# The start of a decoder kernel: constants and first loads as operations of its graph, and low-rank weights in two arrays

## The chip, the core and the metric

The kernel runs on one core of a Trainium2 chip. Its time is the device time of one execution in microseconds, the median of the runs shown. A lower time is better.

## What is computed

The reference is a decoder of four layers on `x` (4 x 256 x 128) with a context (4 x 512 x 96). Twelve stages each add their output to `x`. Two of them stand at the start and are touched by the change: `attn0` (one head of self-attention) and `X0` (cross-attention to the context with 16 heads, low-rank additions to its four weights, and four image tokens with keys and values of their own).

```python
def _L0_xattn_ref(x, context, Wq, Wk, Wv, Wo, bo, q_down, q_up, q_alpha, ...):
    def _lora(t, down, up, alpha):
        return t @ down @ up * (LORA_W * alpha[0] / RANK)
    q_in = x @ Wq + _lora(x, q_down, q_up, q_alpha)
    org_ctx = context[:, :end, :]
    ipa_ctx = context[:, end:, :]
    k_in = org_ctx @ Wk + _lora(org_ctx, k_down, k_up, k_alpha)
    v_in = org_ctx @ Wv + _lora(org_ctx, v_down, v_up, v_alpha)
    out = _attention(q_in, k_in, v_in)
    out = out + IPA_SCALE * _attention(q_in, ipa_ctx @ Wk_ipa, ipa_ctx @ Wv_ipa)
    return out @ Wo + bo + _lora(out, o_down, o_up, o_alpha)
...
    x = x + _L0_attn_ref(_layernorm(x, axis=-1), L0_attn_W, L0_attn_b)
    x = x + _L0_xattn_ref(_layernorm(x, axis=-1), ctx_768, ...)
    x = x + _L0_ffn_ref(_layernorm(x, axis=-1), ...)
    ...
```

The other stages are two feed-forward nets and a mixture of experts, two attentions with small heads, a wide causal attention, an attention from latents, a net with quantised weights, one more single head (`attn3`) and one more wide cross-attention (`X3`), and at the end `F3`, six layers of local attention and feed-forward.

## The kernel before

`Decoder.prepare` and the start of `Net.run` issue by hand, ahead of everything else: the transfers of `x` (four, SP's queue), of `cols`, `rows` and `ctxT` (ACT's queue), of the mask (SP), and on POOL the identity, the causal masks, the band masks, the zeroed tiles `pads`, `vs` and `vb` and the selection pattern `pick16`. `Net.prepare` fills those tiles with memsets.

All else is a graph. A stage calls `op(name, fn, reads, writes, holds)`; the name gives the engine, a weight and a due time from the table `NET` (or `LOCAL` for F3). A planner, `Flow.order`, runs a list schedule: it keeps a time per engine, takes the operation that can start first, and among those that can start takes the one with the earliest due time. The result is one fixed order of instructions for each engine; each engine works its list strictly in that order and waits by semaphores. `LAGS` gives how long an operation's result needs to its readers. Where PE would stand idle for a while, the planner puts in turns of the identity matrix (`keep`), whose result nobody reads; the first such group, `warm`, has `WARM` turns. So three kinds of PE instruction carry line 412: turns of data, keep-warm turns and `warm`.

All working tiles are cut out of one tensor, `arena`, by kinds: `w4` (1024 columns, seven slots) for the wide weights, `x4` (four slots), `e2` (five), `h` (two), `kx`, `qx` and so on. A `fetch` (L426) is a transfer on SP's queue into such a slot, and waits for the slot's last users. Hardware transfers share eight completion semaphores in turn, so the ninth waits for the first.

The head of the order, in words, with the lines of before:

- `n_stats` (DVE, L440 and L441), `n_eps` (DVE, L445), `n_root` (POOL, L446), `n_scale` (DVE, L456, two halves), `n_turn` (PE, L412) and a copy by ACT (L417) make the normalised and turned `x` of a batch.
- `attn0`: `h_qk` and `h_v` (PE, L409), the queries and keys with bias (DVE, L519 and L520), `h_scores`, `h_max` (DVE, L550), `h_exp` (ACT, L557), `h_turn`, `h_weigh`, `h_add` (DVE, L581). `x_bias` (POOL, L495) adds a row of `rows` to `x` before.
- `low_rank`: for each of q, k, v, o one transfer of the wide factor (32 x 1024, a slot of `x4`) and one of the narrow factor (32 x 128 or 32 x 96, a slot of `e2`); `l_scale` (DVE, L832), `l_mm` (PE, L409, 32 rows), `l_add` to the weights (DVE, L850 for q, k, v and L863 for o).
- `image_keys`: two transfers (into `x4`) and `i_kv`, sixteen matmuls of 16 columns each, then `i_out` (ACT) and `p_kimg` (POOL, L664).
- `X0` for each batch: `p_v` (eight matmuls of 512 columns, copied out by ACT and DVE), and for each pair of heads `p_k`, `p_q`, `p_scores`, `p_max` (DVE, L684), `p_exp` (ACT, L686), `p_share` (POOL, L691), `p_turn`, `p_weigh`.

The order in which stages enter the graph is the text `ORDER`; batches of one stage overlap those of the next.

Of the kernel before, what the change touches and what calls it, by code (L numbers as in the profile page):

```python
# [48 lines left out]
    ("x0_qal", 1), ("x0_kal", 1), ("x0_val", 1), ("x0_oal", 1), ("desc", 8),  # L49
# [17 lines left out]
class Decoder:  # L67
# [17 lines left out]
    def prepare(self):  # L85
# [3 lines left out]
        self.cols = c.tile([P, NCOL], F32, tag="cols", name="cols")  # L89
        self.rows = self.early.tile([P, NROW], F32, tag="rows", name="rows")  # L90
        self.x = []
        for b in range(B):
            xb = c.tile([P, 2, D], F32, tag=f"x{b}", name=f"x{b}")
            nc.sync.dma_start(out=xb, in_=self.a["x"][b].rearrange("(t p) d -> p t d", p=P))
            self.x.append(xb)
        self.load(self.cols, "cols", nc.scalar)
        nc.scalar.dma_start(out=self.rows, in_=self.a["rows"].partition_broadcast(P))
        self.ctxT = self.early.tile([CD, B, NCTX], F32, tag="ctxT", name="ctxT")
        for b in range(B):
            nc.scalar.dma_start(out=self.ctxT[:, b, :], in_=self.a["ctxT"][b])  # L100
# [4 lines left out]

        def mask(name, keeps):
            m = self.early.tile([P, 2, S], F32, tag=name, name=name)
            nc.gpsimd.memset(m, 0.0)
            for t in range(2):
                for base, q, k in keeps(t):  # L110

                    nc.gpsimd.affine_select(
                        out=m[:, t, :], in_=m[:, t, :], compare_op=ALU.is_ge, fill=NEG,
                        base=base + q * t * P, pattern=[[k, S]], channel_multiplier=q,
                    )
            return m

        self.causal = mask("causal", lambda t: [(0, 1, -1)])

        self.ident16 = self.early.tile([P, P], BF16, tag="ident16", name="ident16")  # L120
        nc.vector.tensor_copy(self.ident16, self.ident)
        self.causal16 = self.early.tile([P, P], BF16, tag="causal16", name="causal16")
        self.band16 = self.early.tile([P, 2 * P], BF16, tag="band16", name="band16")
        for m, lo, k, q in ((self.causal16, 0, -1, 1), (self.band16, 0, -1, 1), (self.band16, P, 1, -1)):
            m = m[:, lo : lo + P]
            nc.gpsimd.memset(m, 0.0)

            nc.gpsimd.affine_select(
                out=m, in_=m, compare_op=ALU.is_ge, fill=-(2.0**100), base=0, pattern=[[k, P]],
                channel_multiplier=q,  # L130
            )
# [11 lines left out]
class Flow:  # L143
# [22 lines left out]
    SETTLED = 9.0  # L166
# [179 lines left out]
class Net:  # L346
# [72 lines left out]
    def fetch(self, kind, *parts):  # L419
# [3 lines left out]
        def dma():  # L423
            for name, lo, hi, rows, view in parts:
                out = w.t[rows if isinstance(rows, slice) else slice(rows), lo:hi]
                self.nc.sync.dma_start(out=out if view is None else view(out), in_=self.a[name])  # L426

        self.op("fetch", dma, [], [w])
# [63 lines left out]
    def biased(self, b, row, reads=()):  # L492
# [3 lines left out]
            x, x, row()[:, None, :].to_broadcast([P, 2, D])), [self.x[b], *reads], [self.x[b]])  # L496


    def one_head(self, b, w, rows, scale, biased, causal):
# [63 lines left out]
        self.op("h_max", most, [sc], [nmx, pr] if causal else [nmx], [sums, pr])  # L563
# [28 lines left out]
    def pair_weights(self, names, rows):  # L592
        view = lambda x: x.rearrange("p (g m) -> p g m", m=D)
        return {
            m: self.fetch("w4", (name, 0, 1024, rows if m in "kv" else P, view if m == "o" else None))
            for m, name in zip("qkvo", names)
# [35 lines left out]
    def cross_wide(self, stage, w, bias, image=None):  # L632
# [4 lines left out]
        for b in range(B):  # L637
# [3 lines left out]
            v, vmade, vt = self.pair_values(b, w, lambda c, b=b: d.ctxT[:, b, c * P : (c + 1) * P], [], 4)  # L641
# [14 lines left out]
    def cross_pair(self, b, g, w, xT, v, vmade, vt, oT, n, image):  # L656
# [3 lines left out]
        self.op("p_k", lambda: self.mm(pk.t[:, :n], w["k"].t[:CD, cut], d.ctxT[:, b, :n]), [w["k"]], [pk], [kT])  # L660
# [83 lines left out]
    def causal_pair(self, b, g, w, xT, v, vmade, vt, oT):  # L744
# [21 lines left out]
        for e in range(2):  # L766
# [22 lines left out]
            self.op("c_max", masked, [ps2], [prob], [p, nmx])  # L789
# [29 lines left out]
    def low_rank(self, w):  # L819

        nc, d = self.nc, self.d
        parts = {}
        for i, (m, rows) in enumerate((("q", D), ("k", CD), ("v", CD), ("o", RANK))):

            r = slice(RANK * i, RANK * (i + 1))
            low, high = ("down", "up") if m != "o" else ("up", "down")
            n = rows if m != "o" else D
            big = self.fetch("x4", (f"x0_{m}{high}", 0, 1024, r, None))
            small = self.fetch("e2", (f"x0_{m}{low}", 0, n, r, None))

            def scale(m=m, small=small, n=n, r=r):
                nc.vector.tensor_scalar(  # L832
                    small.t[r, :n], small.t[r, :n], d.col(f"x0_{m}al")[r], 1.0 / RANK, ALU.mult, ALU.mult,
                )

            self.op("l_scale", scale, [small], [small])
            parts[m] = big, small, r, rows
        for h in range(2):
            cut = slice(h * 512, (h + 1) * 512)
            made = {m: self.buf("bank") for m in "qkv"}  # L840

            def products(made=made, cut=cut):
                for m, ps in made.items():
                    big, small, r, rows = parts[m]
                    self.mm(ps.t[:rows, :], small.t[r, :rows], big.t[r, cut])

            self.op("l_mm", products, [b for m in "qkv" for b in parts[m][:2]], list(made.values()))
            for m, ps in made.items():
                n = parts[m][3]
                self.op("l_add", lambda m=m, n=n, cut=cut, ps=ps: nc.vector.tensor_add(  # L850
                    w[m].t[:n, cut], w[m].t[:n, cut], ps.t[:n, :]), [ps, w[m]], [w[m]])
        big, small, r, _ = parts["o"]
        for h in range(2):
# [3 lines left out]
            def product(ps=ps, h=h):  # L857
                for i in range(4):
                    g = 4 * h + i
                    self.mm(ps.t[:, i * D : (i + 1) * D], big.t[r, g * P : (g + 1) * P], small.t[r, :D])  # L860
# [5 lines left out]
    def image_keys(self):  # L866

        d, out = self.d, {}
        for m in "kv":
            wi = self.fetch("x4", (f"x0_w{m}i", 0, 1024, CD, None))  # L870
# [10 lines left out]
            self.op("i_kv", product, [wi], [ps])  # L881
# [1827 lines left out]
```

## Time and profile before

| what | us |
|---|---|
| median of 3 runs | 2117.17 (2116.97 to 2117.47) |
| the profiled execution, its own time | 2120.44 |
| span of that execution in the profile | 2118.5 |
| PE busy in the span | 2050.2 (97%) |
| DVE, ACT, POOL busy | 1638.8, 1179.3, 993.1 |
| mean granted clock of TensorE | 0.986 |

The times of a view are those of one execution, from the start of its span. A row of the timeline gives start, length, engine, line, operation, what it writes and reads, shapes and count; the bracket holds the idle time ahead of it and what ended it. A row of the windows gives the stretch, its length, then busy time and count for PE, PEld (weight loads), DVE, ACT and POOL, the granted clock of TensorE (1.00 is full speed), the share of the DMA engines and GB/s. In the chain of waits a row is start, length and what the time went to. An fp32 matmul stands as two instructions in the trace, a turn as one.

### The profile page before, as it was taken

The page shows a single profiled execution, that of the slowest core. Times are in us where ns is not written, and L with a number is a line of the kernel's source. Part 1 is how long each engine was busy: PE and PEld are TensorE (multiplying, and loading weights), DVE is VectorE, ACT ScalarE, POOL GpSimd, SP SyncE. Part 2 cuts the span into 40 slices and gives each one's busy share as a digit, 9 for nine tenths or more (in the row PEclk, how much of TensorE's full clock was granted, in tenths as well). Part 3 has the DMA queues.
Part 4 walks back from the last instruction along what each step waited for, and adds up shares of the span by engine and source line. Part 5 has one row for each costly group of instructions (what it writes and reads, how often), then busy time and mean ns, then how long its engine had stood idle before and what let it go on. Part 6 is the DMA issues. An engine that isn't in the chain of part 4 may idle for free.

```text
span 2118.5 us, 59911 instructions
## 1 busy us (share of the span) xinstructions
PE 2050.2 (97%) x24498; PEld 1373.6 (65%) x24499; DVE 1638.8 (77%) x4352; ACT 1179.3 (56%) x2668; POOL 993.1 (47%) x1155
## 2 busy tenths in 40 slices
PE   8999999999999998899999999999999999999998
PEld 6666675776675666666665666666656666666666
DVE  4767777788787668988887688789788797797882
ACT  2654727344536677566565565556556465556553
POOL 3334415231312245445364357557567465575660
PEclk8999999999999999999999999999999999999999
DMA  5000020111020000100000102112121021211101
GB/s 155 1 1 2 1 70 1 32 40 55 2 76 2 9 2 5 56 3 1 1 1 1 51 13 70 42 31 74 42 72 52 25 70 42 71 46 42 29 23 32
DMA packets 33425, 71.21 MB, mean 34 GB/s; under 512 B 5688, under 2 KB 17984, under 8 KB 33152
## 3 DMA queue, kind: packets, MB, share of 16 engines
q1 hardware_dynamic: 20320, 50.29, 8.0%
q10 hardware_dynamic: 12832, 17.09, 2.5%
q8 instruction: 194, 3.18, 0.6%
q14 instruction: 79, 0.65, 0.1%
HBM read 41.68 MB, written 0.52 MB: 20 GB/s over the span
## 4 chain that ended last, share of the span: by engine, by line
PE 68%; DVE 22%; POOL 5%; issue 3%; ACT 2%; DMA 1%; POOLq 0%; SPq 0%; ACTq 0%; DVEq 0%
PE bank L409 39%; PE bank L1828 17%; PE bank L412 9%; PE bank L2044 2%; DVE arena L1982 2%; DVE arena L1992 2%; DVE arena L1997 2%; POOL arena L2034 2%; DVE arena L1603 1%; POOL arena L1996 1%; POOL arena L2077 1%; PE bank L2118 1%; DVE arena L2085 1%; DVE arena L417 1%; DVE arena L2087 1%
## 5 line engine op out<-in xcount | busy, mean ns | idle before, releaser
L409 PE MATMUL bank<-arena 128*64 128x256 f32 (+11 forms) x6824 | 857.5, 393 | 10.5 <-ACT arena L1525 3.6
L409 PEld LDWEIGHTS bank<-arena 128*128 128x128 f32 (+4 forms) x6824 | 532.6, 165 | 276.8 <-issue 100.0
L1828 PE MATMUL bank<-arena 64*64 64x32 f32 (+3 forms) x13584 | 651.7, 251 | 6.4 <-issue 2.6
L1828 PEld LDWEIGHTS bank<-arena 64*64 64x64 f32 (+2 forms) x13584 | 387.4, 127 | 209.3 <-issue 115.9
L417 ACT COPY arena<-bank 128x512 f32<-128x512 f32 (+4 forms) x586 | 269.6, 489 | 286.1 <-PE bank L409 199.9
L1996 POOL TENSOR_TENSOR arena<-arena 128x1024 f32<-128x1024 f32 x96 | 226.7, 2364 | 124.1 <-PE bank L1828 63.4
L691 POOL TENSOR_SCALAR arena<-arena 128x508 f32<-128x508 f32 (+1 forms) x256 | 176.8, 697 | 209.2 <-DVE arena L688 184.1
L412 PEld LDWEIGHTS bank<-ident,arena 128*128 128x128 f32 x1757 | 196.6, 141 | 116.2 <-issue 47.3
L412 PE MATMUL bank<-ident,arena 128*128 128x128 f32 x1757 | 253.5, 280 | 18.3 <-DVE arena L456 8.5
L686 ACT ACTIVATE arena<-bank,arena 128x508 f32<-128x508 f32 (+1 forms) x256 | 175.3, 691 | 78.6 <-DVE arena L684 36.6
L2034 POOL TENSOR_TENSOR arena<-arena 128x1024 f32<-128x1024 f32 x96 | 180.9, 1905 | 71.8 <-DVE arena L2018 71.8
L1990 ACT ACTIVATE arena<-bank 128x512 f32<-128x512 f32 x192 | 113.9, 601 | 133.2 <-PE bank L1828 105.7
L684 DVE TENSOR_REDUCE arena<-bank 128x1 f32<-128x508 f32 (+1 forms) x256 | 164.2, 676 | 18.6 <-PE bank L409 18.4
L1002 ACT ACTIVATE arena<-bank 128x512 f32<-128x512 f32 (+1 forms) x256 | 124.6, 582 | 63.9 <-PE bank L409 62.4
L417 DVE COPY arena<-bank 128x512 f32<-128x512 f32 (+1 forms) x196 | 125.8, 667 | 42.9 <-PE bank L412 27.7
L1992 DVE TENSOR_TENSOR arena<-bank,arena 128x512 f32<-128x512 f32 x192 | 127.5, 683 | 38.0 <-ACT arena L1990 36.4
L2077 POOL TENSOR_TENSOR arena<-arena 128x1024 f32<-128x1024 f32 x48 | 91.4, 1904 | 108.5 <-ACT arena L2050 62.7
L1982 DVE TENSOR_TENSOR arena<-bank,arena 128x256 f32<-128x256 f32 x384 | 138.4, 411 | 3.1 <-ACT arena L1990 2.7
L979 DVE TENSOR_REDUCE arena<-bank 128x1 f32<-128x512 f32 (+2 forms) x256 | 116.7, 513 | 21.5 <-PE bank L409 21.1
L2050 ACT COPY arena<-bank 128x512 f32<-128x512 f32 x192 | 103.3, 601 | 28.8 <-PE bank L2044 28.7
L1997 DVE TENSOR_REDUCE arena<-arena 128x16 f32<-128x1024 f32 x96 | 114.3, 1201 | 0.0
L2044 PEld LDWEIGHTS bank<-ident,arena 128*128 128x128 f32 x768 | 87.0, 142 | 42.0 <-POOL arena L2034 21.8
(230 smaller groups left out, 2460.7 us busy)
## 6 DMA issues: line engine op xcount, KB each, us to landing
arena<-arena SPq DMA_DIRECT2D x48, 384.0 KB, 3.9
arena<-in_f_w SPq DMA_DIRECT2D x24, 512.0 KB, 3.5
arena<-in_f_wqkv ACTq DMA_DIRECT2D x18, 512.0 KB, 7.0
arena<-arena SPq DMA_DIRECT2D x48, 128.0 KB, 2.3
arena<-in_f_wo ACTq DMA_DIRECT2D x6, 512.0 KB, 4.0
arena<-in_f_w ACTq DMA_DIRECT2D x6, 341.0 KB, 3.9
arena<-in_f_w ACTq DMA_DIRECT2D x6, 192.0 KB, 6.2
arena<-in_x_wq SPq DMA_DIRECT2D x2, 512.0 KB
```

The costliest lines, as they stand in the source:

```text
L409: self.nc.tensor.matmul(out, lhsT, rhs, start=start, stop=stop)
L412: self.nc.tensor.transpose(out, in_, self.d.ident)
L417: return self.op(name, lambda: copy(out(), in_()), reads, writes, holds)
L684: self.op("p_max", lambda ps=ps, one=one: nc.vector.tensor_reduce(one(nmx), ps.t[:, :n], AX.X, ALU.max, negate=True), [ps], [most], [nmx])
L686: self.op("p_exp", lambda ps=ps, one=one, cols=cols: nc.scalar.activation(cols(), ps.t[:, :n], AF.Exp, bias=one(nmx), accum_out=one(sums)) ...
L691: nc.gpsimd.tensor_scalar(cols(), cols(), one(sums), 1.0, ALU.mult, ALU.mult)
L1828: self.nc.tensor.matmul(out, lhsT, rhs, start=start, stop=stop)
L1982: nc.vector.tensor_mul(heads(tmp.t[:, cut])[:, :, lo : lo + 32], heads(ps.t)[:, :, 32 - lo : 64 - lo], spread(1, lo, lo + 32),)
L1992: op("cosine", lambda cut=cut, ps=ps: nc.vector.tensor_mul(heads(out.t[:, cut]), heads(ps.t), spread(0, 0, 64)), [ps, w["tab"]], [out])
L1996: op("rotary", lambda: nc.gpsimd.tensor_add(out.t, out.t, tmp.t), [out, tmp], [out])
L1997: op("norms", lambda: nc.vector.tensor_reduce(ss.t[:, at : at + 16], heads(sq.t), AX.X, ALU.add), [sq], [ss])
L2034: nc.gpsimd.tensor_mul(heads(out.t), heads(out.t), rs.t[:, at : at + 16, None].to_broadcast([P, 16, 64]))
```

## The change

1. The transfers of `x`, `rows`, `ctxT` and the mask and the filling of the constants on POOL become operations of the graph (`load_x`, `load_rows`, `load_ctx`, `load_mask`, `k_causal`, `k_ident`, `k_masks`, `k_pads`, `k_values`, `k_image`, `k_pick`). The filling operations read a buffer that the `load_x` operations write, so the planner places them behind those; readers of the constants name them as buffers they read.
2. The first fetches get names and due times of their own (`load_a`, `load_low`, `load_ups`, `load_wk`, `load_ctx0`, `load_wv`, `load_wq`, `load_ctx`, `load_rows`, `load_image`, `load_wo`), with weights after their bytes. All but `cols` go to SP's queue.
3. The eight low-rank factors come in two arrays, `x0_ups` (128 x 1024) and `x0_downs` (128 x 128), with the four alphas in one column; one `l_scale` scales all four. The factors keep their 32 rows each.
4. `WARM` goes from 34 to 20, `SETTLED` from 9.0 to 8.0, and all due times of both tables and the two paces are set anew by small amounts.

```diff
-        self.x = []
-        for b in range(B):
-            ...
-            nc.sync.dma_start(out=xb, in_=self.a["x"][b].rearrange("(t p) d -> p t d", p=P))
-        self.load(self.cols, "cols", nc.scalar)
-        nc.scalar.dma_start(out=self.rows, in_=self.a["rows"].partition_broadcast(P))
-        for b in range(B):
-            nc.scalar.dma_start(out=self.ctxT[:, b, :], in_=self.a["ctxT"][b])
+        self.load(self.cols, "cols", nc.scalar)
+    def load_x(self, b):
+        self.nc.sync.dma_start(out=self.x[b], in_=self.a["x"][b].rearrange("(t p) d -> p t d", p=P))
+    def load_rows(self):
+        self.nc.sync.dma_start(out=self.rows, in_=self.a["rows"].partition_broadcast(P))
+    def load_context(self, b):
+        self.nc.sync.dma_start(out=self.ctxT[:, b, :], in_=self.a["ctxT"][b])
...
+        at = {m: slice(RANK * i, RANK * (i + 1)) for i, m in enumerate("qkvo")}
+        big = self.fetch("x4", ("x0_ups", 0, 1024, P, None), name="load_ups")
+        small = self.fetch("h", ("x0_downs", 0, D, P, None), name="load_low")
+        self.op("l_scale", lambda: nc.vector.tensor_scalar(
+            small.t[:, :D], small.t[:, :D], d.col("x0_al"), 1.0 / RANK, ALU.mult, ALU.mult), [small], [small])
...
+        begun = Buffer()
+        for b in range(B):
+            self.op("load_x", lambda b=b: d.load_x(b), [], [self.x[b], begun])
+            self.op("load_ctx" if b else "load_ctx0", lambda b=b: d.load_context(b), [], [self.context[b]])
+        self.op("load_rows", d.load_rows, [], [self.rows])
+        self.op("k_causal", d.fill_causal, [begun], [self.causal])
+        self.op("k_ident", lambda: nc.vector.tensor_copy(d.ident16, d.ident), [begun], [self.masks])
+        self.op("k_masks", d.fill_masks, [begun], [self.masks])
...
+        self.op("k_pads", empty, [begun], [b for bufs in pads.values() for b in bufs])
+        self.op("k_values", values, [begun], [self.fixed("vs", self.vss) for _ in self.vss])
+        self.op("k_image", image, [begun], [self.fixed("vb", self.vbs) for _ in self.vbs])
+        self.op("k_pick", pick, [begun], [self.pick])
+        self.op("load_mask", mask, [], [self.pick])
...
+    "load_a": ("SP", 0.8, -900.0),
+    "load_x": ("SP", 0.55, -800.0),
+    "load_low": ("SP", 0.3, -700.0),
+    "load_ups": ("SP", 2.05, -690.0),
+    "load_wk": ("SP", 1.55, -600.0),
+    "load_ctx0": ("SP", 0.8, -540.0),
+    "load_wv": ("SP", 1.55, -500.0),
+    "load_wq": ("SP", 2.05, -400.0),
+    "load_ctx": ("SP", 0.8, -300.0),
+    "load_rows": ("SP", 1.55, -250.0),
+    "load_image": ("SP", 1.55, -200.0),
+    "load_wo": ("SP", 2.05, -150.0),
+    "load_mask": ("SP", 0.9, 30.0),
+    "k_causal": ("POOL", 1.4, 43.74),
...
-LAGS = {"fetch": 6.0, "constants": 4.0, "weights": 12.0, "spread": 3.5}
+LAGS = {**{k: 2.0 for k in NET if k[:5] == "load_"}, "fetch": 6.0, "constants": 4.0, "weights": 12.0, "spread": 3.5}
...
-WARM = 34
+WARM = 20
```

The instruction lists that follow from it are these at the head. SP: `a_w`, four `x`, `x0_downs`, `x0_ups`, `x0_wk`, the first `ctxT`, `x0_wv`, `x0_wq`, three `ctxT`, `rows`, `x0_wki`, `x0_wvi`, `x0_wo`, the mask, F0's weights. POOL: the identity, `n_root` of the first batch, then memsets of `pads` (four), `vs` (two, each followed by a strided one on it, which after is L1081), `vb` (two), the masks, `pick`, the causal mask, then `x_bias`. PE: 20 warm turns, `n_turn`, `h_qk`, `l_mm` (k, v, q, first half), `l_mm` (o), `h_scores`, `l_mm` second half and o, `h_v`, one `p_k`, `h_turn`, four `p_v`, `h_weigh`, `i_kv` for k and v, three `p_v`, `n_turn` for X0, one `p_v`, one `p_k`, three `p_q`, the first `p_scores`. Before, the order was `n_turn`, `h_qk`, `h_v`, `h_scores`, 21 keep-warm turns, `h_turn`, `l_mm` both halves, `h_weigh`, 24 keep-warm turns, `l_mm` for o, `i_kv`, one `p_k`, `n_turn`, two `p_v`, one `p_q`, one `p_v`, the first `p_scores`.

## The prediction, made before the changed kernel had run

> **What bounds the kernel now.** I read the page first. TensorE fills the span, and its chain carries most of it:
>
> ```profile
> span 2118.5 us, 59911 instructions
> PE   8999999999999998899999999999999999999998
> PE 68%; DVE 22%; POOL 5%; issue 3%; ACT 2%; DMA 1%; POOLq 0%; SPq 0%; ACTq 0%; DVEq 0%
> ```
>
> The reader should see one weak slice at the start (8), two in the middle, one at the end. The change edits the start, so I read the timeline of PE from 0 to 42 us next:
>
> ```profile
> 1.59 5.92 PE L412 MATMUL bank<-ident 128*128 128x128 f32 x34 [1.59 <-POOL ident masks.py:199]
> 10.04 0.33 PE L412 MATMUL bank<-ident,arena 128*128 128x128 f32 x1 [2.52 <-DVE arena L456]
> 11.53 4.17 PE L409 MATMUL bank<-arena 128*128 128x256 f32 x12 [0.46 <-ACT arena L417]
> 15.49 2.69 PE L412 MATMUL bank<-ident 128*128 128x128 f32 x21
> 20.03 3.65 PE L409 MATMUL bank<-arena 32*128 32x512 f32 x20 [1.42 <-DVE arena L832]
> 23.51 2.78 PE L412 MATMUL bank<-ident 128*128 128x128 f32 x24
> 27.15 2.05 PE L409 MATMUL bank<-arena 32*128 32x128 f32 x16 [0.85 <-DVE arena L832]
> 29.12 8.48 PE L409 MATMUL bank<-ctxT,arena 96*128 96x16 f32 x34
> 41.94 0.70 PE L409 MATMUL bank<-arena 64*128 64x512 f32 x2
> ```
>
> The x34, x21 and x24 rows turn only the identity: keep-warm work that nobody needs. The first useful matmul is at 10.04, the low-rank products at 20.03 and 27.15, the first X0 scores at 41.94. The chain of waits for that window says why:
>
> ```profile
> 2.30 5.86 DMA x<-in_x
> 8.19 3.94 DMA ctxT<-in_ctxT
> 12.14 7.54 DMA arena<-in_x_qdown
> 19.70 0.28 DVE arena L832
> 27.15 10.45 PE bank L409 x50
> ```
>
> Transfers end three waits in a row; `q_down`, 16 KB, lands 7.54 us after its issue because the large weights stand before it. Then DVE and the windows of 3.41 us:
>
> ```profile
> 4.48 4.02 DVE L445 TENSOR_SCALAR arena<-arena 128x2 f32<-128x2 f32 x1
> 26.20:29.61 3.41, 2.56 (x22) 2.35 (x21) 3.31 (x12) 0.00 (x0) 2.12 (x3) 1.00 1.00 361
> 29.61:33.03 3.42, 3.42 (x19) 3.42 (x18) 1.11 (x2) 0.27 (x1) 0.36 (x3) 0.50 0.55 194
> 39.85:81.80 41.95, 41.95 (x222) 23.96 (x223) 29.20 (x87) 27.53 (x67) 14.91 (x44) 1.00 0.00 1
> ```
>
> L445 has a median of 159 ns over its 56 runs; here it takes 4.02 us, until POOL's run of memsets (3.85 to 8.48) pauses. The granted clock is 0.50 from 29.61 to 39.85, beside 16-column matmuls. From 39.85 to 81.80 PE is busy throughout: a loss before that is a loss at the end.
>
> **What moves in the instruction lists.** Without identity fills both kernels issue the same 14099 matmul operations. The first 201 hold the same set in another order (the 201st is reached at 81.8 us before); then the order is identical up to the 561st, and 84% of all stand in the same place. Rearranged pieces lie mainly between the 5327th and 6743rd (1192 to 1383 us) and in the last 5%. So the price is the head, carried to the end.
>
> **The head, step by step** (durations from rows of before).
> *Transfers.* Before, a_w was issued only at 6.72. Now it goes first, then four x, downs and ups: none of these seven on SP waits. Sizes in this order: a_w and cols 244 KB, x 512, downs 64, ups 512, wk 384, ctx0 192, wv 384, wq 512, three ctx 576, rows 384, wki 384, wvi 384. Before moved 137 GB/s over 0–5 us and 264 to 280 over 5–15; cumulated at these rates: downs at 5.6 us, ups 7.6, wk 9.1, wv 11.3, wq 13.2, rows 16.7, wvi 19.5.
> *First x.* Before it started DVE at 3.54, first in its queue. Behind a_w (one issue, 0.45, and 192 KB) I take 4.2; four BN rows (0.94) and L445 (0.16): 5.3. POOL is now free there: n_root 0.72, done 5.97 (before 9.30).
> *The new cover problem.* All the fills now stand directly behind n_root on POOL: four memsets of 0.25, one of 0.91, then L1081, which waits for that memset and leaves a gap. n_scale is the same kind of DVE operation that stood 4.02 us at L445. Bounds: not held, done at 7.1; held through the whole chain of fills (their rows sum to 10 us), done near 17. Value: DVE enters at gaps, as it did between the pick selects (9.34 to 10.68), so one half at 8.1, the other at the next gap, 9.3 (before 10.68). What waits for n_scale is the turn, ACT's copy and all of PE. l_scale stands behind it on DVE and gets the gap at 10.6.
> [...]
> *PE.* h_qk from 10.1 (before 11.53). The warm-up is 20 instead of 34; at 0.213 us each it ends at 5.9, PE is nearly idle until 8.1, and I expect the clock at 0.50 from 9.1 to 12.5 (before 12.5 to 16.0): h_qk 1.7, ends 11.8. Then at full clock: low-rank products half 1 with part at half clock 1.4, o-part 0.9 (8 x 0.112), scores 0.86, half 2 1.0, o-part 0.9, h_v 0.45, p_k 0.86: 18.3 with small waits for DVE. DVE beside it: l_add 0.69 each, h_max 0.69; v's last l_add ends 17.9, so the first p_v at 18.75 is just covered; a later one moves PE one for one. Then turn 0.44, four p_v 3.4, weigh 0.9: 23.1. i_kv: 32 x 0.112 = 3.6 at full clock, to 26.7; wki and wvi landed by 19.5, so 3.6 to 7 us of cover.
> DVE adds to x, takes two statistics (to 25.8), POOL copies image keys after the first i_out (25.3 to 26.0) and does two n_root (27.4); n_scale 29.1, turn 29.3, one p_v, one p_k, three p_q (0.43 each); **first scores at 32.6**, before 41.94.
> *Equal work.* Ahead of its first scores the new order has done one p_k, five p_v and two p_q more: 0.86 + 4.3 + 0.86 = 6.0 us. So 32.6 compares with 41.94 + 6.0 = 47.9: a lead of 15.3.
> *Deductions.* The clock fell after the window that held the 32-row products and stayed at 0.50 through the 16-column ones, though PE shows as busy. i_kv now fills a window of its own: one more at 0.50 costs 1.7; at least none, at most three (5.1). I take one.
> [...]
> First softmaxes now start without the stock of p_v that PE had at 42–48: some idle, 0 to 2, taken 0.6. Lead: 15.3 - 1.7 - 0.6 = **13.0 us**.
> *Edits at nothing.* Three l_scale fewer (0.26 each): DVE waited for q_down anyway. The mask transfer waits on DVE until after h_add, near 23 us, and holds F0's weights behind it on SP; before they were issued at 23.18 too and F0's first operation (L1168) stood at 117.3. x_bias waits for rows at 16.7 behind POOL's fills (to 16.1), h_add needs it at 23: cover 6. Masks, pick and causal are used only in later stages. ACT loses five issues and loads its table at once.
> *The rest.* Retuned due times move pieces in 1192–1383 us, where PE idles 7.8 us per 200. Either sign; rows say nothing on it, so -3 to +3, taken 0.
>
> **The sum.** The profiled execution took 2120.44 (span 2118.5), 3.3 above the median 2117.17. After: 2107.4 by the profiled one, and 2117.17 - 13.0 = **2104.2**. A measurement of this kernel can tell some 0.2%, 4.2 us, from no change.
>
> **Rivals.**
> 1. *DVE is held by the whole chain of fills* (row L445 for it, the pick selects against): h_qk moves from 10.1 to 17; lead 13 - 7 = 6: 2111. Chance 0.10.
> 2. *PE stays at half clock through the head*, as the 45 fills that are gone there no longer feed it: two windows more, 3.4, and up to 2 of waits: lead 8: 2109. For it: 1.68 busy of 3.42 at 9.13 was followed by 0.50. Chance 0.09.
> 3. *The lead is spent*: where DVE paces (800–900 us, DVE 92%, PE 88%), an early PE waits longer. Against: all engines keep their order there, so all shift. About 2117. Chance 0.06.
> 4. *Slower*: the rearranged piece at 1192–1383 opens a stall per repeated step. The longest wait of PE there now is 4.4 us (behind DVE L456). It decides from four such: 2104.2 + 17.6 = 2121.8, 0.2% over the median of before; six give 2130.6. The PE lists are mostly local swaps: chance 0.05.
> The forecast keeps 0.70.
>
> **Range.** Low: n_scale not held (1.8), no extra slow window (1.7), no first idle (0.6), late pieces 1 of their 3: 13 + 5 = 18, 2099. High: it must take in rivals 1 and 2, 2111, with late pieces up: 2112.5. Outside: rivals 3 and 4 and the forecast's edges, under 0.2. Faster by over 0.2% means below 2112.9: forecast and rivals 1 and 2 less tails, 0.86; within, 0.08; slower, 0.06.
>
> **What would show it.** n_root's first at 5.3; the second n_scale ending near 9.3 (17 means rival 1); h_qk near 10; no wait for a low-rank transfer; first scores at 31 to 35; clock 0.50 in two windows of the first 40 us; the rows from 100 us on shifted evenly by 11 to 15 us. A PE idle that is new after 400 us, or first scores after 40, makes me wrong.

## The result and the profile after

The changed kernel took 2104.93 us (median of 6 executions, 2100.16 to 2111.98); six more in a later comparison gave 2108.14 (2105.21 to 2111.57). The ratios to the executions of before that ran beside them are 0.9937 [0.9919, 0.9956] and 0.9951 [0.9933, 0.9970]: by the medians, faster by 10 to 13 us. The profiled execution took 2104.31.

The executions of one program lie up to 15 us apart (12 for the changed kernel), and the time goes with the mean granted clock that each execution lists. Over all 170 executions of this study, with one level for each kernel, 0.001 of mean clock is worth 1.56 us, and 1.3 us remain as scatter. The last column moves each kernel's mean to a clock of 0.990 by this slope (about 1 either way; 0.3 for before): an estimate, called "equal clock" below. Two limits go with it. The mean clock is made of the half-clock windows on record; a slow start ahead of the first record of an execution (at 13.91 us in the profile below) is not in it. And an edit can move the clock itself, which this column then takes out of the edit's effect.

| kernel | n | median | ratio, 95% | mean clock | equal clock |
|---|---|---|---|---|---|
| before (all comparisons) | 72 | 2116.94 | | 0.9884 | 2115.1 |
| changed | 6 | 2104.93 | 0.9937 [0.9919, 0.9956] | 0.9910 | 2106.4 |
| changed, again | 6 | 2108.14 | 0.9951 [0.9933, 0.9970] | 0.9897 | 2107.7 |
| before + new due times | 10 | 2119.01 | 1.0005 [0.9989, 1.0020] | 0.9859 | 2111.7 |
| changed, old due times | 10 | 2109.80 | 0.9968 [0.9956, 0.9979] | 0.9893 | 2108.9 |
| constants not released by x | 8 | 2108.45 | 0.9963 [0.9951, 0.9974] | 0.9901 | 2109.2 |
| transfers in graph order | 10 | 2120.22 | 1.0022 [1.0008, 1.0036] | 0.9900 | 2121.1 |
| eight low-rank transfers | 4 | 2106.62 | 0.9950 [0.9935, 0.9965] | 0.9905 | 2107.2 |
| warm-up 34 | 10 | 2112.40 | 0.9972 [0.9961, 0.9983] | 0.9887 | 2110.2 |
| constants after n_scale | 4 | 2107.77 | 0.9950 [0.9931, 0.9969] | 0.9888 | 2104.9 |
| image transfers late | 6 | 2110.22 | 0.9958 [0.9942, 0.9975] | 0.9890 | 2107.3 |
| x1 to x3 late | 6 | 2104.93 | 0.9931 [0.9914, 0.9947] | 0.9900 | 2104.5 |
| low-rank factors late | 6 | 2108.95 | 0.9949 [0.9932, 0.9966] | 0.9897 | 2107.8 |
| contexts and rows first | 12 | 2115.40 | 0.9985 [0.9971, 1.0000] | 0.9882 | 2111.9 |

Three rows tell how rough the last column is: "constants after n_scale" has the instruction lists of the changed kernel but for one cast of 0.2 us on DVE, and the three read 2106.4, 2107.7 and 2104.9. So a difference of 2 in equal clock is weak evidence where nothing else goes with it.

The page after, with the same three lines as before: the weak first slice (8) is a 9 now, and the chain's share for transfers has gone from 1% to 0%.

```profile
span 2102.6 us, 59813 instructions
PE   9999999999999999899999998999999999999998
PE 68%; DVE 22%; POOL 5%; issue 3%; ACT 2%; DMA 0%; POOLq 0%; ACTq 0%; SPq 0%; DVEq 0%
```

PE's timeline after: the warm-up, then the useful rows that matter here. No x21 or x24 of keep-warm turns is left; the first useful turn stands at 8.03 (before 10.04), the low-rank products are inside the x36 from 11.3 on (before 20.03).

```profile
1.58 4.53 PE L413 MATMUL bank<-ident 128*128 128x128 f32 x20 [1.58 <-POOL ident masks.py:199]
8.03 0.69 PE L413 MATMUL bank<-ident,arena 128*128 128x128 f32 x2 [1.92 <-DVE arena L457]
9.19 6.64 PE L410 MATMUL bank<-arena 128*128 128x256 f32 x36 [0.46 <-ACT arena L418]
23.29 3.71 PE L410 MATMUL bank<-ctxT,arena 96*128 96x16 f32 x32 [0.71 <-PE bank L410]
```

The chain of waits after (start, length, what). Of the three transfers that it held before, one is left, the first x; behind it the chain is PE with pieces of DVE, POOL and ACT. But "issue" at 22.59 is a wait in disguise: PE stood 0.70 before the image products, which came free when wki landed (issued at 12.72, 10.5 to landing).

```profile
1.25 2.73 DMA x<-in_x
6.01 1.98 DVE arena L457
9.19 2.07 PE bank L410 x4
11.29 3.44 PE bank L410 x12
22.59 0.70 issue
23.29 8.08 PE bank L410 x38
```

The windows after (stretch, length, busy time and count of PE, PEld, DVE, ACT, POOL, clock, DMA share, GB/s). From 3.7 to 20 us the transfers run at 233 to 247 GB/s with the DMA engines nearly or fully busy (shares of 0.89 to 1.06), as in the first row. A full share is not one rate, though: the third row has 386 at 1.01. The window that the image products fill (the second) is followed by one at half clock.

```profile
7.10:10.49 3.39, 1.99 (x5) 1.42 (x6) 2.04 (x3) 0.37 (x1) 3.25 (x7) 1.00 1.01 233
24.15:27.56 3.41, 3.41 (x28) 3.17 (x28) 1.16 (x9) 0.53 (x2) 1.98 (x7) 1.00 0.76 259
27.56:30.97 3.41, 3.41 (x5) 1.22 (x4) 2.44 (x7) 0.00 (x0) 0.76 (x2) 0.50 1.01 386
```

The clock column reads 1.00 wherever the profile has no record, and here the first record is at 13.91. That PE ran at half until then is read from the durations: the 20 turns took 4.53, 0.23 each, where the x24 of before took 2.78, 0.12 each; and h_qk's four instructions took 2.07, 0.52 each, where the 18 of the same shape from 33.14 on, at a recorded full clock, took 4.24, 0.24 each.

The first X0 scores start at 34.53 (before 41.94). With the 6.0 us of work that the new order has ahead of them, that is a lead of 13.4; the lead is by how much earlier than in before the same operation stands. To follow the lead further I matched DVE's and POOL's operations of the two traces one by one and took the median difference in each stretch:

| time of before, us | 100–200 | 300–500 | 500–700 | 850–900 | 950–1050 | 1150–1200 | 1300–1350 | 1500–1700 | 1900–2000 | 2050– |
|---|---|---|---|---|---|---|---|---|---|---|
| lead of after | 12.8 | 13.0 | 13.0 | 14.3 | 15.9 | 19.1 | 16.8 | 16.9 | 18.5 | 16.1 |

What the head won by 100 us is still there at 700. The steps up behind that, and the last one down, go with half-clock windows which the one execution had at that place and the other not; the second profile of the same program stands at 14.9 from 100 to 200 and at 15.3 at the end. The step down from 19.1 to 16.8 is none of these: before has three half-clock windows there (1292.54 to 1302.78) and after one (at 1270.01). It lies in the rearranged piece. From 1180–1235 to 1345–1400 the lead falls by 2.1, in the second profile by 1.9, with the old due times (experiment 1) also by 1.9, and in all twelve profiles with the new graph by 0.5 to 3.6; with the new due times in the kernel before it rises by 0.8. So the new order of that piece gives some 2 us of the lead back, and it comes with the new graph, not with the retuning.

### The profile page after: what moved, and what is told of

Same layout as the page of the kernel before. It is cut to its first block, busy times and chain, and to the rows that moved or that the text cites. A ratio compares the mean times of both kernels' runs of the same rounds, so it can differ in the third digit from the quotient of the medians.

```text
span 2102.6 us, 59813 instructions
## 1 busy us (share of the span) xinstructions
PE 2033.9 (97%) x24449; PEld 1360.3 (65%) x24450; DVE 1636.5 (78%) x4349; ACT 1178.0 (56%) x2668; POOL 991.8 (47%) x1155
## 4 chain that ended last, share of the span: by engine, by line
PE 68%; DVE 22%; POOL 5%; issue 3%; ACT 2%; DMA 0%; POOLq 0%; ACTq 0%; SPq 0%; DVEq 0%
PE bank L410 38%; PE bank L1846 17%; PE bank L413 9%; PE bank L2062 2%; DVE arena L2000 2%; DVE arena L2010 2%; DVE arena L2015 2%; POOL arena L2052 2%; DVE arena L1639 1%; POOL arena L2014 1%; PE bank L2136 1%; DVE arena L2103 1%; DVE arena L2105 1%; POOL arena L2095 1%; DVE arena L2035 1%
## 5 line engine op out<-in xcount | busy, mean ns | idle before, releaser
L418 ACT COPY arena<-bank 128x256 f32<-128x256 f32 (+3 forms) x586 | 269.6, 489 | 269.2 <-PE bank L410 179.4
L413 PE MATMUL bank<-ident,arena 128*128 128x128 f32 x1757 | 254.1, 280 | 19.3 <-DVE arena L457 8.2
L2062 PE MATMUL bank<-ident,arena 128*128 128x128 f32 x768 | 101.7, 278 | 16.4 <-POOL arena L2052 16.4
```

Of the source, the lines that this page charges most:

```text
L413: self.nc.tensor.transpose(out, in_, self.d.ident)
L418: return self.op(name, lambda: copy(out(), in_()), reads, writes, holds)
L2062: nc.tensor.transpose(ps.t[:, i * P : (i + 1) * P], out.t[:, (g + i) * P : (g + i + 1) * P], d.ident)
```

## The experiments

My theory: the gain is made in the first 40 us by what comes first, and is carried to the end. The rivals put it on the retuned late pieces (A), on the released constants or the two arrays alone (B to D), or hold that only the bytes ahead of the last early transfer count (H).

### 1. Due times alone, and the change without them

First the kernel before with the new numbers, then the changed kernel with the old ones, for all names that both have (paces, patience and some 200 due times).

```diff
-    "h_qk": ("PE", 0.87, -17.12),
+    "h_qk": ("PE", 0.87, -17.03),
...
-NET_PACE = 1.177894
+NET_PACE = 1.175628
```

> The kernel before with only the retuned due times and paces of the names that both kernels share. Its TensorE order is that of before up to the 560th matmul; the last 10% stands as in the changed kernel. Theory (the gain is made in the first 40 us, by transfers in the order of use and by constants behind the first x): no gain, 2118 with 3 us either way, and the same operation stands within 1.5 us of before at 100 to 200 us. Rival A (the retuned late pieces make the gain): 2105 to 2109, with the lead growing only in the last tenth of the span.

> The changed kernel with the due times and paces of before for the names that both share; the new operations keep theirs. The head has the new transfers and constants, the last 10% has the order of before. Theory: first X0 scores at 34.5 within 1.5, operations at 100 to 200 us stand 12 to 14 us earlier than before, time 2105 within 4. Rival A (late pieces): 2113 to 2118, although the head leads.

Due times alone gave 2119.01, ratio 1.0005: no gain in time, as the theory had it. But its mean clock is the lowest of all, and in equal clock it stands 3.4 below before, which the theory did not have. Its lead at 100 to 200 us is -2.2, outside the 1.5 that I had given, although TensorE's order there is that of before: it had five half-clock windows in the head where the profile of before had four (up to 1.7 us each, an estimate: half of a window's 3.41). The change without them kept most of the gain (2109.80), but less than all: first scores at 38.0 instead of the 34.5 I expected, lead 11.1, outside my 12 to 14. With the old numbers h_weigh comes behind the image products, at 30.33 instead of 21.52, so the second norm is late, and PE stands 0.62 for its n_scale at 36.2 where the changed kernel has no wait:

```profile
30.33 1.06 PE L410 MATMUL bank<-arena 128*128 128x128 f32 x8
36.19 0.58 PE L413 MATMUL bank<-ident,arena 128*128 128x128 f32 x2 [0.62 <-DVE arena L457]
```

So the retuning is worth nothing by the medians of the first run, and 1.8 (in the second) to 3.4 (in the first) in equal clock; which of these holds is not settled. The part that the trace shows lies in the head. Rival A falls as the cause of the whole: without the new due times 6.2 of the 8.0 in equal clock remain.

### 2. Constants not released by x

```diff
-        self.op("k_causal", d.fill_causal, [begun], [self.causal])
+        self.op("k_causal", d.fill_causal, [], [self.causal])
...
```

(and the same for the other six fills)

> The changed kernel with the constants not released by the load of x: POOL's fills start at once and stand ahead of n_root, transfers as in the changed kernel. Theory (constants behind the first n_root are a part of the gain): n_root ends after the fills, at 12 to 14 instead of 5.97; PE begins with the low-rank products near 11.5 to 13 instead of h_qk at 9.2; operations at 100 to 200 us lead by 8 to 11 instead of 12.8, the time is 2 to 5 us above the changed kernel. Rival B (the transfers alone make the head, constants are covered by them): lead 12 to 13, time within 1 of the changed kernel in equal clock.

Median 2108.45; 2.1 above the changed kernel in equal clock (the mean of its two rows, 2107.1), lead 10.5: inside the theory's bounds, the time at their edge. POOL's timeline and PE's show both halves of the mechanism: n_root waits for 10.6 us of fills, and PE starts with the low-rank products instead, when ups lands.

```profile
12.05 0.72 POOL L447 TENSOR_TENSOR arena<-arena,neghalf 128x2 f32<-128x2 f32 x1
10.64 3.80 PE L410 MATMUL bank<-arena 32*96 32x512 f32 x28 [4.52 <-DMA arena<-in_x_ups]
```

A delay of n_root by nearly 7 us is thus only some 2 in lead and in equal clock, since PE had other work to put first. The intervals of the ratios overlap, so that the place of the constants is a part of the gain is supported by both numbers and not shown beyond doubt.

### 3. All first transfers in the order of the graph

```diff
-    "load_a": ("SP", 0.8, -900.0),
-    "load_x": ("SP", 0.55, -800.0),
...
+    "load_a": ("SP", 0.3, -130.03),
+    "load_x": ("SP", 0.3, -130.03),
...
```

> The changed kernel with one due time, weight and lag for all first transfers (those of the old fetch), so that they go in the order of the graph: x, contexts, rows, mask, a_w, downs, ups, wk, wv, wq, wo, wki, wvi. Two arrays and released constants stay. Theory (the order of the transfers is the larger part): ups land near 12 to 13, the first useful matmul at 12 to 14 instead of 9.2, operations at 100 to 200 us lead by 4 to 8 instead of 12.8, time 2109 to 2114. Rival C (released constants or two arrays make the head, the order of transfers is hidden): lead 11 to 13, time 2104 to 2107.

2120.22: slower than before by 0.22% [0.08%, 0.36%], lead -4.0 at 100 to 200 us. The sign is the theory's, the size twice what I had given. PE's timeline shows why: 82 turns of warm-up and keep-warm, then one piece of products, then 6 us for the l_add of wo, which the planner had put ahead in DVE's list and whose transfer landed at 20.43.

```profile
1.58 11.11 PE L413 MATMUL bank<-ident 128*128 128x128 f32 x82 [1.58 <-POOL ident masks.py:199]
13.98 2.07 PE L410 MATMUL bank<-arena 32*96 32x512 f32 x28 [1.29 <-DMA arena<-in_x_ups]
22.08 6.98 PE L410 MATMUL bank<-ctxT,arena 96*128 96x16 f32 x32 [6.03 <-DVE arena L844]
```

The clock was at half from 19.3 to 32.9; the 32 instructions of the last row took 0.22 each, where those of the changed kernel took 0.12 (3.71 in all). Two arrays, constants as operations and one queue, without the order, are worse than the kernel before. But the run changes more than the transfers: with these due times and the longer lag the planner put the fills ahead of n_root again, and attn0 behind the image products. n_root on POOL and the first turn of x on PE:

```profile
12.03 0.72 POOL L447 TENSOR_TENSOR arena<-arena,neghalf 128x2 f32<-128x2 f32 x1
35.26 0.38 PE L413 MATMUL bank<-ident,arena 128*128 128x128 f32 x2
```

The late n_root alone was worth some 2 in experiment 2; how the other 12 (in equal clock) divide between the transfers and the order on PE is not shown.

### 4. Eight low-rank transfers into the same two tiles

```diff
-        big = self.fetch("x4", ("x0_ups", 0, 1024, P, None), name="load_ups")
+        big = self.fetch("x4", *((f"x0_{m}up", 0, 1024, at[m], None) for m in "qkvo"), name="load_ups")
```

(and the same for the downs)

> The changed kernel with the low-rank factors in eight transfers again (four downs, four ups, issued back to back where the two stood) into the same two tiles; TensorE's order is identical. One issue takes SP 0.43 to 0.47, so six more put wk and all later transfers 2.8 later in issue. Theory (order and bytes matter, the count does not, since the transfers' rate ends the waits): ups land 0 to 1.5 later than 11.15, lead at 100 to 200 us 11 to 13 over before (the changed kernel 12.77), time 2104 to 2108. Rival D (two arrays are a large part of the gain): first matmul of the products at 14 or later, lead under 10, time over 2109.

2106.62, in equal clock as the changed kernel; lead 13.2. An effect of the count of transfers is not measurable: rival D falls. My "0 to 1.5 later" was wrong in sign, the products started earlier (at 9.67 instead of 11.29), but see the landings below: they differ as much between executions of one program.

### 5. The warm-up of before

`WARM = 34` instead of 20.

> The changed kernel with the warm-up of 34 turns of before instead of 20; nothing else, TensorE's order is identical. In the changed kernel the granted clock stays at half until 13.9. Theory E (the shorter warm-up is too short to raise the clock; it costs half of what TensorE does from 9.2 to 13.9, of which the wait for ups covers a part): full clock from about 9, lead 13.3 to 14.5 instead of 12.77, time 1 us lower in equal clock. Rival (the first full clock depends on the steady work after 10 us): clock at half to 13 or later, lead 12.3 to 13.

The clock did as theory E had it at first, full from 5.9 on (h_qk took 1.13 instead of 2.07), and the products, with ups landed at 9.5, were done 3 us sooner; then it fell to half (0.50) from 23.0 to 33.2, three windows where the first profile of the changed kernel had one. The lead is 11.3, outside both expectations, and the time 3 above in equal clock. Two windows of it:

```profile
9.35:12.76 3.41, 3.22 (x33) 2.67 (x32) 2.25 (x4) 0.14 (x1) 3.12 (x11) 1.00 1.01 251
23.00:26.41 3.41, 3.41 (x19) 3.41 (x18) 0.33 (x3) 0.27 (x1) 2.02 (x7) 0.50 0.90 281
```

### 6. Constants behind n_scale

`begun` is the buffer that the first norm writes, instead of that of `load_x`.

> The changed kernel with the constants released by the first n_scale instead of the first load of x: POOL's fills begin after n_scale; TensorE's order is identical. [...] Rival (n_scale is on the chain that sets the head): lead 13.9 or more.

The edit did not do what it was made for. A buffer of the planner sets the order of the lists and no wait; POOL's list stayed as it was, and the fills still began 0.08 us ahead of n_scale. n_scale took 0.62 all the same, not 2.04, and so it did in four other runs whose POOL list was the changed kernel's. It is a race that goes either way: over the ten profiles with these fills beside n_scale, it took 2.03 to 2.04 in five and 0.62 in five. So by chance this profile has what the edit was to give, h_qk at 7.45 instead of 9.19 (my estimate for it was 7.6 to 8.2, with a lead of 12.8 to 13.4), and its lead is 12.2, short of the 13.9 that the rival asked for. With three half-clock windows in this head that is a sign against the rival and no more. Here the chain of waits shows a transfer, wv, as the end of a wait (as in the kernels of experiments 4 and 5):

```profile
7.45 1.13 PE L410 MATMUL bank<-arena 128*128 128x256 f32 x4 [0.46 <-ACT arena L418]
5.17 8.37 DMA arena<-in_x_wv
```

The two operations of the race in the timeline of the changed kernel's first profile:

```profile
5.93 1.06 POOL L1075 MEMSET arena<- 128x256 f32 x4
6.01 2.04 DVE L457 TENSOR_SCALAR arena<-x,arena 128x128 f32<-128x128 f32 x2 [0.78 <-POOL arena L447]
```

and in that of the kernel with eight transfers, in the same order and with the same 0.08 between them:

```profile
5.83 1.21 POOL L1075 MEMSET arena<- 128x256 f32 x4
5.91 0.62 DVE L457 TENSOR_SCALAR arena<-x,arena 128x128 f32<-128x128 f32 x2 [0.78 <-POOL arena L447]
```

In the first DVE took 1.42 us longer, in the second POOL took 0.15 longer.

### 7. Image transfers behind wo

`load_image` gets a due time of -140 instead of -200. The planner then splits the two image products and runs them later.

> The changed kernel with the two image transfers behind wo (2.1 us later); the scheduler then puts the two 16-column products (i_kv) 3 and 4 pieces later and apart, each between 512-column pieces. Theory F (a window of 3.41 us filled by 16-column products is granted half clock next; and i_kv's wait of 0.71 was for its transfer): no half-clock window at 27 to 31, no wait of i_kv, lead 14 to 15.3 instead of 12.77, time 1.5 to 2.5 lower in equal clock. Rival G (the half-clock window comes from the end of the warm part whatever is run, or the transfer's delay costs TensorE one for one): lead 10.7 to 13.

Lead 10.2, below both expectations, and 2107.3 in equal clock, the changed kernel's time. What theory F told did not come: the half clock came all the same, for two windows. But the edit did not take away its condition, since 2.6 us of both products still fell into one window; the theory stays untested. PE no longer waited for wki. Two windows, the first with most of both image products in it, busy throughout:

```profile
26.95:30.36 3.41, 3.41 (x27) 2.93 (x26) 2.82 (x13) 0.85 (x2) 1.74 (x7) 1.00 0.65 202
30.36:33.77 3.41, 3.41 (x6) 1.50 (x6) 1.91 (x6) 0.85 (x2) 1.77 (x3) 0.50 0.94 341
```

### 8. The changed kernel again, factors late, x late

> The changed kernel once more, unaltered, for a narrower ratio and to see what differs between two executions of one program. Theory (the spread comes from where the 3.41 us windows of the granted clock fall on the program): median 2103 to 2109, each execution's time following its mean granted clock by about 1.5 us per 0.001; the landing of ups between 8.5 and 11.7, since it differed that much between executions with the same transfers ahead of it. Rival (the profiled execution is typical): first full clock at 13.9, ups at 11.15, one half-clock window at 804 to 900 of before, as in the first profile.

The theory on the spread held: 2108.14 at clock 0.9897, first full clock elsewhere, three half-clock windows between 804 and 900 of before instead of one, and none behind the image products.

The low-rank factors behind wk, a context, wv and wq (`load_low` and `load_ups` at -350 and -340):

> The changed kernel with the low-rank factors behind wk, the first context, wv and wq (1.47 MB later); the set of transfers, and what stands ahead of wki, is the same. Theory (what counts is which bytes come first): ups land near 16 to 17, the low-rank products begin there instead of at 11.3, and TensorE has only one head's pieces to put ahead: lead 7 to 10 instead of 12.8, time 3 to 6 above the changed kernel in equal clock. Rival H (wki is the bound, the order among the earlier transfers is hidden): lead 12 to 13.

The products began at 15.95, as told, and the lead of 9.6 to 10.4 at 100 to 200 us is near the theory's; but that profile had three half-clock windows in the head, and the time, 2107.8 in equal clock, is 0.7 above the changed kernel and not 3 to 6. PE had h_qk, h_v and h_scores to run meanwhile. So in time rival H is right here: the place of the factors within the first 2.8 MB is nearly hidden.

x of batches 1 to 3 later, with the edit of experiment 6:

```diff
+    "load_x1": ("SP", 0.55, -350.0),
+    "load_x2": ("SP", 0.55, -220.0),
+    "load_x3": ("SP", 0.55, -210.0),
...
-    "load_ups": ("SP", 2.05, -690.0),
-    "load_wk": ("SP", 1.55, -600.0),
+    "load_ups": ("SP", 3.6, -690.0),
+    "load_wk": ("SP", 1.0, -600.0),
```

> The changed kernel with two edits: constants released by the first n_scale, and x of batches 1 to 3 issued later (x1 behind wq, x2 and x3 behind rows), so that 384 KB fewer stand ahead of the low-rank factors; the scheduler's weights of ups and wk are set so that TensorE's order stays but for i_kv, one piece later. Theory (transfers, in the order of use, end the waits of the head): at 236 to 245 GB/s the factors and wk, wv land 1.1 to 1.6 earlier, lead at 100 to 200 us 13 to 15 where the clock has as much half-clock time as in the changed kernel (1.7 us of TensorE after 20 us), time in equal clock 1 to 2 below the changed kernel. Rival H (wki's landing at 23.2, which all bytes ahead of it set, is the bound): lead 12 to 13, time in equal clock within 1 of the changed kernel.

2104.93, ratio 0.9931 [0.9914, 0.9947], and 2.6 below the changed kernel in equal clock, with a lead of 13.0 although n_scale took 2.04 here. Ratio and equal clock are the lowest of all, but the interval overlaps that of the changed kernel, and the kernel of experiment 6, whose edit is in this one too, stands only 0.4 higher in equal clock: that it is better is not shown.

### 9. Contexts and rows first

```diff
-    "load_a": ("SP", 0.8, -900.0),
-    "load_ctx0": ("SP", 0.8, -540.0),
+    "load_a": ("SP", 0.8, -710.0),
+    "load_ctx0": ("SP", 0.8, -790.0),
...
```

> The changed kernel with the four contexts and rows (1.15 MB) right behind x, and a_w behind them; then downs, ups, wk, wv, wq, wki, wvi, wo. The bytes ahead of wki are the same as in the changed kernel. In the run with all transfers in the order of the graph a_w was issued only at 10.81 and ups landed at 13.98. Theory (what is used first must come first: a_w and the factors with nothing large ahead): a_w issued near 9 to 11, h_qk at 13 to 15 instead of 9.2, products at 16 to 17.5, lead at 100 to 200 us 6.5 to 9.5 (two executions of the changed kernel: 12.8 and 14.9), time in equal clock 3 to 6 above the changed kernel. Rival H (only the bytes ahead of wki count, the order among the earlier ones is hidden, as where the factors alone came 1.47 MB later and the time rose by 2 or less): lead 11.5 to 15, time in equal clock within 1.5 of the changed kernel.

2115.40, ratio 0.9985 [0.9971, 1.0000]: by the medians nearly the whole gain is gone, in equal clock 4.9 of 8.0; lead 9.1. The same bytes stand ahead of wki, so rival H falls here. One premise of what I had expected was misread: the transfer issued at 10.81 in experiment 3 was that of wq; a_w was issued at 5.93 there, and at 5.22 here instead of 9 to 11. It landed 7.1 later. In the timeline h_qk waits for a_w:

```profile
12.48 1.55 PE L410 MATMUL bank<-arena 128*128 128x256 f32 x8 [3.01 <-DMA arena<-in_a_w]
```

and in the chain of waits the next end is set by wq, 12.08 us from its issue:

```profile
8.16 12.08 DMA arena<-in_x_wq
```

With experiments 2, 3 and 8 this points to the larger part: what must come early is what TensorE can start on (a_w, then the weights of q, k and v), and with 1.15 MB in front of it, of which TensorE reads nothing before 16 us, more than half of the gain goes. Where the factors stand among the early ones hardly matters. One thing is not taken apart: the planner answered the new due times with another order on PE here too (h_weigh at 31.18 instead of 21.52, the turn for X0 at 36.73 instead of 31.21), and a run with these transfers and the PE order of the changed kernel was not made.

## Why the prediction was right

The forecast of 2104.2 was met (2104.93, and 2105.8 as the median of all twelve), the range held both medians, and a lead of 13.0, one extra half-clock window (in the first profile) and the lead's survival to the end came as told. The mechanism held: transfers in the order of use and constants out of the way of the first norm give a lead in the first 40 us, which lasts. That the number fits so well is in part luck. Inside, several terms were off and cancelled:

- **Transfers: mis-sized.** I took 264 to 280 GB/s from before; the windows show 233 to 247 with the DMA engines nearly or fully busy. ups landed at 11.15 instead of 7.6. rows came at 21.85 instead of 16.7, and wki at 23.2, when PE already stood waiting for it: of the covers of 6 and of 3.6 to 7 us none was left, and PE paid 0.71. That no product waited for ups, as told, hung on h_qk at half clock, which ended at 11.26; in other profiles PE waited 0.61 and 3.00 for it. The transfers had become a bound beside PE up to 23 us.
- **n_scale: mechanism half right.** n_root was done at 5.98 (5.97). Both halves of n_scale passed in the gap after 7.9, 8.05 in all, not 8.1 and 9.3; h_qk stood at 9.19, 0.9 earlier than told. I had taken DVE's loss for certain; over the ten profiles with these fills beside n_scale it came in five. The rows of experiment 6 show the same order, POOL first by 0.08, with either end (2.04 and 0.62). The 1.8 that the low end of the range has for an n_scale not held is shown by no run; in experiment 6, where n_scale took 0.62, h_qk stood 1.74 earlier, and the lead was 12.2.
- **Clock: place wrong, sum near.** Half clock from 9.1 to 12.5 was told; in the profile PE ran at half until 13.9. There the 20 turns of the warm-up took 4.53 and the clock was still at half behind them; in the second profile they took 3.71, so it had risen before they ended, and it fell back at 7.7. h_qk took 2.07 instead of 1.7.
- **First scores:** told at 32.6 and 1.7 for the window, 34.3; measured 34.53.
- **The rest, taken as 0 within 3:** the two parts have opposite signs. The retuning was worth 0 to 3.4 (experiment 1); the rearranged piece at 1192 to 1383 us took some 2 of the lead back.
- **Missing: the mean clock.** Of the raw difference (means 2117.6 and 2106.5, 11.1), 8.0 remain in equal clock; the mean clock rose from 0.9884 to 0.9903. Fewer half-clock windows in the head are a part of that (four in the profile of before; in those of after one, behind a start at half clock to 13.9, and two).

Rivals: the chain of fills did not hold DVE (8.05, not 17). Half clock in the head came in part. The lead was not spent from 800 on. Rival 4 came small: at 1192 to 1383 us the lead goes from 19.1 to 16.8, with waits of PE no longer than 1.95 (before 2.07), so no stall of 4.4 per step.

## What to carry to other kernels

Sort the first transfers by what the bound engine can start on, and count them at the rate that these transfers show when the DMA engines are all busy (233 to 247 GB/s here): with 1.15 MB of later operands in front of the first ones, more than half of what the change brought was gone, a new order on PE included. Look at what order the planner makes of an edit of due times before its effect is put down to the transfers. A loss on one engine's list (n_root 7 us late, the products 4.7 late) shrank to a third or less in equal clock where TensorE has other pieces to put first. Before a few us are ascribed to an edit, run one program twice: here the executions of the changed kernel lie 12 us apart, and the mean granted clock tells what part of a difference may be the clock's (1.56 us per 0.001 here).

## What the runs showed of the hardware

**The clock's windows have a phase.** All half-clock stretches, but those cut off by the end of a trace, are multiples of 3.413 us (3.413, 6.827 and 10.240 in the profile of before) on one grid, and the grid lies differently on the program in each execution. Between 770 and 920 us of before all kernels run nearly the same order. Put in the time of before (start plus the lead just ahead of this stretch), the phase of the grid sorts the 14 profiles by how many half-clock windows they got there. The bounds of the rows were drawn with the counts in view:

| phase, us | profiles | half-clock windows |
|---|---|---|
| 0.20 to 0.40 | changed; image late; factors late | 1, 1, 1 |
| 0.52 to 1.03 | constants free; due times alone; constants after; contexts first; warm-up 34; eight transfers | 4, 5, 4, 4, 4, 4 |
| 1.58 to 2.23 | x late; graph order | 2, 2 |
| 2.31 to 3.32 | before; changed again; old due times | 3, 3, 4 |

Each costs up to 1.7 us, an estimate: half of 3.41. Over all 170 executions the mean clock goes with four fifths (0.81) of the spread between executions of one kernel (by variance), so windows of this kind are where most of it lies. A window of the changed kernel there:

```profile
789.38:796.21 6.83, 5.35 (x36) 4.51 (x36) 6.06 (x20) 6.42 (x21) 3.94 (x5) 1.00 0.00 1
```

and the same stretch of the eight-transfer kernel, at the same lead within 0.2 us:

```profile
789.38:796.21 6.83, 5.90 (x15) 4.72 (x16) 4.12 (x17) 4.59 (x15) 4.10 (x5) 0.50 0.00 1
```

Half clock came straight behind a busy window: the rows 24.15:27.56 and 26.95:30.36 were busy throughout (3.41 of 3.41) and were followed by 0.50. In ten profiles a window at full clock with 2.3 us or more of 16-column products was followed by half clock (in nine of them PE was busy throughout), and in the second run of the changed kernel two with 1.9 and 1.8 were not; the second of them:

```profile
24.79:28.20 3.41, 3.41 (x21) 2.49 (x21) 1.68 (x8) 0.53 (x2) 2.02 (x7) 1.00 0.82 270
```

With the warm-up of 34 a window with 1.6 was followed by half clock, but PE was idle for 0.7 in it. Some of these stretches lasted one window, some two or more. What is counted stays open.

**One transfer lands at different times.** rows is issued when ups has landed (at 11.18 and 11.15 in the first profile), since it takes over that completion semaphore: rows, wki, wvi, wo and the mask each waited there for the transfer eight places ahead (2.1, 1.2, 0.5, 1.3 and 1.8 us). In seven executions with the same seven transfers on SP ahead of ups' landing (a_w, four x, downs, ups, issued at the same times within 0.03) it was issued at 9.08, 9.50, 9.87, 10.52, 10.82, 11.18 and 11.55. Why is not shown. SP's timeline of the kernel with constants after n_scale:

```profile
9.08 0.35 SPq L108 DMA_DIRECT2D rows<-in_rows  x1
```

and of the changed kernel, first profile:

```profile
11.18 0.35 SPq L108 DMA_DIRECT2D rows<-in_rows  x1
```
